# Attention over the scales: the second projection of k and the first of v between the spreads of factors and of weights

## The chip, the cores and the metric

The kernel runs on one core of one Trainium2 chip. The metric is the time of one execution on the device, in microseconds (us). Of the kernel before three executions were timed: the median is 5141.35 us, the lowest 5138.96, the highest 5146.54. Everything is float32.

The engines are named as in the profile: PE is TensorE (matmuls, PEld its weight loads), DVE is VectorE, ACT is ScalarE, POOL is GpSimd.

## What is computed

Four layers follow each other on an image of 2 x 128 channels x 64 x 64: a state-space block with its feed-forward part, two self-attentions over the image's positions, and last an attention over four scales. The change touches this last layer alone. Cut to what matters:

```python
SCALES = (1, 2, 4, 8)
feats = []                                   # four maps of 128 channels, 64 x 64
for i, scale in enumerate(SCALES):
    xs = x if scale == 1 else mean over scale x scale blocks of x
    f = conv3x3(xs, conv_w[i], conv_b[i])
    feats.append(f if scale == 1 else bilinear_resize(f, 64, 64))
xr = stack(feats) as (positions, 4, 128)
q, k, v = split(xr @ attn_in_w.T + attn_in_b)          # 8 heads of 16 channels
attn = softmax(q @ k.T / sqrt(16))                     # 4 x 4 per position and head
o = (attn @ v) @ attn_out_w.T + attn_out_b
res = o + xr
normed = (res - mean(res)) * rsqrt(var(res) + eps) * ln_g + ln_b
out = fus_w @ (the four scales of normed, 512 channels) + fus_b
```

At each of the 8192 positions, four vectors of 128 channels attend to each other, are normalised, and are fused into one.

## The kernel before

The last layer works on items of 512 positions: 2 images x 8 = 16 items. Channels lie on the 128 partitions, positions along the free dimension. The instructions are issued in the order of the program text, each engine works through its own queue in that order, and an engine waits only where it needs what another one has not yet done.

**Items and periods.** `period(n, extra)` is called for n from -2 to 16. One period handles four items at once, each at another step of its way: o = n-1 is fused and written out, p = n gets its weighted sum of v, its output projection and its normalisation factors, m = n+1 gets its scores and its softmax, r = n+2 gets its features, its convolution and its q. What a step does:

- `features(r)` (POOL) builds the three resized scales of `f`; `conv(r, taps)` (PE) and `conv_out(r)` (ACT) build scale 0, in nine matmuls into `pf`.
- `project(i, which, si)` (PE) is one matmul of 128 x 128 by 512 into a buffer `pqkv`. For q (0) and v (2) ACT then copies it to SBUF with its bias; for k (1) it stays in PSUM until `product` reads it. The two k of scales 0 and 1 are made at the end of the period ahead, those of scales 2 and 3 inside this one.
- `product(m, ti)` (DVE) multiplies k of scale ti with q of all four scales into `prod`; `scores(m, ti)` (PE) sums it over the channels of each head into `psc`; `soft_max`, `soft_exp`, `soft_sum` (DVE, ACT, DVE) make the attention weights `at`.
- `weights(p, ti)` (PE, eight short matmuls of 32 rows) spreads the weights of scale ti over the channels into `pw`; `weighted(p, ti)` (DVE) multiplies them with v of scale ti into `ov`; `add_ov` adds the four up (one on POOL, two on DVE).
- `mix_out(p, si)` (PE, then ACT) makes `po`, and from it `sq` and `cen`; `variance` (PE, ACT) and `newton` (DVE, ACT, DVE) make the factors `rs`; `factors(p)` (PE, eight short matmuls of 32 rows) spreads them over the channels into `prs`; `normalise` (DVE, in the next period, where the item is o) multiplies `cen` with them; `fuse(o, ...)` (PE) makes `pfus`, which ACT and a DMA write out as `ot`.

**PSUM.** The eight banks are full. Three hold `mm`, the buffers of one bank that `pqkv`, `pf`, `po` and `pfus` share in turn; one holds `acc` (`psc` and `pva`); four hold the single buffer of tag `pw`, in which `pw` and `prs` replace each other: the weights of an item can be spread only when `normalise` has read the factors of the item ahead. A buffer of a tag is given out again in the order in which the program gave it back.

**SBUF.** v of an item is one tile of 4 x 512 numbers per partition, with one buffer for all items. `prod`, `ov` and `sq` share six buffers.

**The order around the change.** At the end of a period PE does `variance`, then q of scales 0 to 3 of item r, then k of scales 0 and 1 of item r, then `factors(p)`. The next period (in which r has become m, and p has become o) starts on DVE with `product(m, 0)` and `normalise(o)`, on PE with `weights(p, 0)`, k of scale 2, and the first half of `fuse(o)`. The first projection of v stands behind the last scores and `soft_max`, ahead of the last five taps of `conv`; the other three follow the convolution. Some periods carry extra work for the second image: `means` in period 2, coarse convolutions in 3 and 4, `columns` in 5.

In the kernel before, the lines of the profile are these: 1032 is the matmul of `project`, 1039 its copy on ACT, 1045 `product`, 1052 `scores`, 1062 to 1080 the softmax, 1087 `weights`, 1094 `weighted`, 1098 `add_ov`, 1107 and 1108 `mix_out`, 1116 `variance`, 1129 and 1131 `newton`, 1138 `factors`, 1145 `normalise`, 1152 `fuse`, 1005 `conv`. Behind the changed places the line numbers of the kernel after are higher by four.

## Time and profile before

| what | before |
|---|---|
| time, median of three | 5141.35 us |
| span of the profiled execution | 5141.6 us |
| PE busy | 4702.8 us (91%) |
| DVE busy | 4093.2 us (80%) |
| ACT busy | 2367.5 us (46%) |
| POOL busy | 2313.1 us (45%) |
| last layer, 4300 to 5141 us: PE, DVE, ACT, POOL busy | 743.5, 539.5, 242.1, 213.3 us of 841 |
| one `normalise` (DVE, 128 x 2048) | 2.28 us |
| one `product` (DVE, 128 x 2048) | 2.35 us |
| one copy of v (ACT, 128 x 512) | 0.69 us |

Busy time is time in which an engine had an instruction under way. A matmul of float32 appears as two records, one for each pass. The profile also gives the clock granted to PE, as a share of full speed: over the whole span it is 0.941, and in the last layer it is whole or half, in stretches of 3.41 us or multiples of that.

There is one `normalise` in each period, so that the distance from one to the next is the length of a period. In the timeline of DVE they start at 4412.54, 4457.56, 4511.39 (with `means`), 4572.97 and 4624.89 (with coarse convolutions), 4678.66 (with `columns`), 4725.40, 4772.66, 4818.52, 4863.55, 4909.37, 4955.34, 5000.37, 5046.19 and 5087.69 us; the last stands at 5128.94.

### The profile page before, as it was taken

The numbers are of one execution on the slowest core, as the hardware profiler recorded it, in microseconds if no ns is written. First come the engines' busy times: TensorE is split into PE (matmuls) and PEld (weight loads), VectorE is DVE, ScalarE is ACT, GpSimd is POOL, SyncE is SP. The second block draws the span as 40 slices with busy tenths as digits, with TensorE's granted clock in tenths as the row PEclk, the third lists the DMA queues.
The fourth block names the chain that finished last, engine by engine and source line by source line (L and its number), as shares of the span: only waits on it lengthen the run. The fifth ranks groups of instructions, "written<-read, shape, count | busy, mean of one in ns | idle before, by whom it ended". The sixth has DMA issues, their size and how long they took to land.

```text
span 5141.6 us, 48961 instructions
## 1 busy us (share of the span) xinstructions
PE 4702.8 (91%) x14797; PEld 2255.8 (44%) x14797; DVE 4093.2 (80%) x4416; ACT 2367.5 (46%) x3221; POOL 2313.1 (45%) x1948
## 2 busy tenths in 40 slices
PE   5889999999888998789999999999999998899997
PEld 1222222222222222356666666666656665333332
DVE  5999999999999999588878887667767774757665
ACT  4677777777777777322221222333333331232332
POOL 2777777767767777313332233333333333222320
PEclk8898889888999988899999999999999999999998
DMA  5333333333222333124443244444444441000000
GB/s 151 72 68 69 67 69 71 71 71 69 67 68 67 71 73 71 33 63 104 103 105 88 70 103 104 117 99 111 111 99 99 112 112 46 5 5 7 7 5 8
DMA packets 237015, 373.85 MB, mean 73 GB/s; under 512 B 88000, under 2 KB 88400, under 8 KB 228432
## 3 DMA queue, kind: packets, MB, share of 16 engines
q1 hardware_dynamic: 187600, 303.55, 24.9%
q10 hardware_dynamic: 49152, 67.17, 5.5%
q8 instruction: 118, 1.93, 0.2%
q14 instruction: 145, 1.19, 0.1%
HBM read 92.18 MB, written 9.83 MB: 20 GB/s over the span
## 4 chain that ended last, share of the span: by engine, by line
PE 45%; POOL 21%; DVE 13%; issue 11%; ACT 4%; DMA 3%; SPq 2%; ACTq 0%; DVEq 0%; POOLq 0%
POOL h L387 17%; PE po L759 13%; PE pq L709 13%; DVE tr L739 3%; PE pf L1005 2%; DMA pt<-tr 2%; SPq L750 2%; PE pqkv L1032 2%; PE py L399 2%; PE pw L1087 1%; POOL z L410 1%; POOL dtu L347 1%; PE psc L1052 1%; DVE h L384 1%; PE pfus L1152 1%
## 5 line engine op out<-in xcount | busy, mean ns | idle before, releaser
L746 POOL COPY pt<-tr 32x512 f32<-32x512 f32 x1024 | 652.6, 637 | 1499.1 <-DVE tr L739 766.8
L384 DVE TENSOR_TENSOR_SCAN h<-da,carry,h 128x512 f32<-128x512 f32 x1024 | 1241.5, 1266 | 59.1 <-ACT da L373 30.2
L387 POOL TENSOR_TENSOR h<-h,cb 128x2048 f32<-128x2048 f32 x256 | 1161.0, 4535 | 20.9 <-POOL carry L386 0.2
L709 PE MATMUL pq<-k,q 128*128 128x512 f32 x2048 | 963.9, 594 | 8.6 <-DVE sc L714 6.2
L759 PE MATMUL po<-pt,vt 128*128 128x256 f32 x4096 | 967.3, 379 | 2.4 <-DMA pt<-tr 2.4
L724 ACT ACTIVATE sc<-sc,nm 128x2048 f32<-128x2048 f32 x256 | 510.5, 1995 | 925.7 <-DVE nm L720 662.3
L714 DVE TENSOR_SCALAR_CACHE_REDUCE sc<-pq 128x1024 f32<-128x1024 f32 x512 | 624.9, 1222 | 361.5 <-PE pq L709 339.9
L759 PEld LDWEIGHTS po<-pt,vt 128*128 128x128 f32 x4096 | 779.1, 190 | 295.2 <-issue 211.3
L373 ACT ACTIVATE da<-dtb,am 128x512 f32<-128x512 f32 x1024 | 681.5, 684 | 222.4 <-DVE h L384 211.4
L739 DVE STREAM_TRANSPOSE tr<-sc 128x2048 f32<-128x2048 f32 x256 | 591.6, 2311 | 68.5 <-DMA pt<-tr 61.8
L366 DVE TENSOR_TENSOR h<-bb,pdu 128x2048 f32<-128x2048 f32 x256 | 581.7, 2272 | 77.4 <-PE py L399 29.3
L399 PE MATMUL py<-h,sel 128*32 128x512 f32 x2048 | 510.8, 642 | 1.6 <-POOL h L387 1.6
L709 PEld LDWEIGHTS pq<-k,q 128*128 128x128 f32 x2048 | 383.6, 190 | 286.7 <-issue 247.7
L360 PE MATMUL pdu<-dtu,fsel 128*128 128x512 f32 x512 | 327.0, 725 | 101.7 <-DVE h L366 101.6
L399 PEld LDWEIGHTS py<-h,sel 128*32 128x32 f32 x2048 | 115.0, 117 | 416.0 <-issue 409.2
L288 PE MATMUL pu<-xn,wu 128*128 128x512 f32 x512 | 244.7, 611 | 2.6 <-ACT xn L278 1.7
L360 PEld LDWEIGHTS pdu<-dtu,fsel 128*128 128x128 f32 x512 | 96.3, 215 | 310.2 <-DVE h L366 186.2
L386 POOL COPY carry<-h 128x4 f32<-128x4 f32 x256 | 47.9, 187 | 387.7 <-DVE h L384 385.9
L1032 PE MATMUL pqkv<-f,ws 128*128 128x512 f32 x384 | 196.0, 636 | 12.3 <-ACT q L1039 6.3
L1094 DVE TENSOR_TENSOR ov<-v,pw 128x2048 f32<-128x2048 f32 x64 | 146.2, 2284 | 60.9 <-PE pw L1087 60.8
L1098 POOL TENSOR_TENSOR ov<-ov 128x2048 f32<-128x2048 f32 x16 | 72.7, 4541 | 253.7 <-DVE ov L1094 253.7
L1016 POOL TENSOR_SCALAR f<-lo 128x256 f32<-128x256 f32 x32 | 27.7, 865 | 324.6 <-PE po L1107 269.6
(241 smaller groups left out, 5408.5 us busy)
## 6 DMA issues: line engine op xcount, KB each, us to landing
pt<-tr SPq DMA_DIRECT2D x2048, 64.0 KB, 2.0
dtb<-dt SPq DMA_DIRECT2D x1024, 64.0 KB, 2.0
pt<-tr ACTq DMA_DIRECT2D x1024, 64.0 KB, 2.2
bb<-dr SPq DMA_DIRECT2D x128, 256.0 KB, 4.7
cb<-dr SPq DMA_DIRECT2D x128, 256.0 KB, 7.7
uw<-ufold SPq DMA_DIRECT2D x14, 576.0 KB, 3.8
xt<-in_x SPq DMA_DIRECT2D x16, 256.0 KB, 5.0
xr<-in_x SPq DMA_DIRECT2D x16, 256.0 KB, 2.9
```

Source lines behind the costliest of these rows:

```text
L360: nc.tensor.matmul(pdu, lhsT=four(s_ % 4), rhs=st[i]["dtu"][:, s_ // 4, :], start=True, stop=True)
L366: nc.vector.tensor_tensor(h, st[i]["bc", 0], pdu.unsqueeze(1).to_broadcast([P, 4, CH]), ALU.mult)
L373: nc.scalar.activation(da, st[i]["dtb", s_], AF.Exp, scale=am[items[i][1]][:, j, gg, m : m + 1])
L384: nc.vector.tensor_tensor_scan(h[:, m, :], da, h[:, m, :], carries[b, l][:, j, gg, m : m + 1], ALU.mult, ALU.add)
L387: nc.gpsimd.tensor_tensor(h, h, st[i]["bc", 1], ALU.mult)
L399: nc.tensor.matmul(py[r : r + 32, :], lhsT=sel, rhs=st[i]["h", s_ + k][:, m, :], start=(m == 0), stop=(m == 3), tile_position=(0, r),)
L709: nc.tensor.matmul(pq[:, i, :], lhsT=st["q", r, grp][:, it * P : (it + 1) * P], rhs=st["k"][:, at : at + CH], start=True, stop=True)
L714: nc.vector.tensor_scalar(dst, pq, 1.0, None, ALU.mult, ALU.max, accum_out=st["mx"][:, c2 : c2 + 1])
L724: nc.scalar.activation(sc, sc, AF.Exp, bias=nm, scale=scale, accum_out=sm[:, hh : hh + 1])
L739: nc.vector.transpose(tr, st.pop(("sc", r, blk, hh)).rearrange("p (t r f) -> p r t f", r=NB, f=32))
L746: nc.gpsimd.tensor_copy(dst, src)
L759: nc.tensor.matmul(st["po", r, grp], lhsT=st["vt"][:, jt, :], rhs=rhs, start=(jt == 0), stop=(jt == N // P - 1))
```

## The change

PE's work stays the same, matmul for matmul; two of them move into the stretch between `factors` of one item and the first `weights` of the next. `factors(p)` now stands ahead of k of scale 1, and v of scale 0 of item m is made at the very start of the period. Since v of scale 0 is then written while all four v of the item ahead are still to be read, v becomes four tiles of 512 numbers with five buffers in all. To save room in SBUF, the maximum of the softmax shares its buffer with the sum.

```diff
@@ project
             name = "qkv"[m]
+            if m == 2:
+                v = st[i]["v", si] = sp.tile([P, CH], F32, name="v", tag="v", bufs=5)
+                nc.scalar.activation(v, pq, AF.Identity, bias=v1("attn_in_b", m))
+                return
             if si == 0:
                 st[i][name] = sp.tile([P, NS, CH], F32, name=name, tag=name)
@@ soft_max
-            mx = sp.tile([P, G4], F32, name="mx4", tag="mx4")
+            mx = sp.tile([P, G4], F32, name="mx4", tag="sm4")
@@ weighted
-            v = st[i]["v"][:, ti : ti + 1, :].to_broadcast([P, NS, CH])
+            v = st[i].pop(("v", ti)).unsqueeze(1).to_broadcast([P, NS, CH])
@@ period
             do(r, features)
+            do(m, project, 2, 0)
             for ti in range(NS):
                 do(m, product, ti)
...
             do(m, soft_max)
-            do(m, project, 2, 0)
             do(r, conv, (4, 5, 6, 7, 8))
...
             do(r, project, 1, 0)
+            do(p, factors)
             do(r, project, 1, 1)
-            do(p, factors)
             more(6)
```

## The prediction

> **What bounds the kernel now.** I read the page first for the engines' shares, then the chain of waits within one period of the last stage, the timeline of TensorE (PE) and VectorE (DVE) over the same period, and last the windows view cut at the edges of the clock records. Only the last stage is touched (from 4299 us on, 842 us of the span); everything ahead of it stays. Page, part 1:

> ```profile
> PE 4702.8 (91%) x14797; PEld 2255.8 (44%) x14797; DVE 4093.2 (80%) x4416; ACT 2367.5 (46%) x3221; POOL 2313.1 (45%) x1948
> ```

> PE is the busiest, but that is a mean over four stages. The chain of waits from 4405 to 4465 us (start, length, engine, tile, line) shows one period of this stage:

> ```profile
> 4409.08 1.16 ACT q L1039 x2
> 4410.25 0.03 issue
> 4410.27 2.35 DVE prod L1045
> 4412.62 2.20 DVE cen L1145
> 4414.83 0.04 issue
> 4414.87 1.18 PE pw L1087 x8
> ...
> 4420.68 1.13 PE pqkv L1032 x2
> ...
> 4432.68 0.99 PE psc L1052 x8
> 4433.68 1.06 PE pqkv L1032 x2
> 4434.73 4.29 PE pf L1005 x10
> 4439.02 2.58 PE pqkv L1032 x6
> ```

> The chain leaves PE for 4.6 us only: q's last eviction on ScalarE (ACT) lets DVE do product 0 and then `normalise` (cen), and only then may the first `weights` run, because pw and prs share one buffer. From 4420.68 on PE carries it without a break to the next q. The row at 4433.68 is v0 (two records: each f32 matmul is two passes); it is on the chain. The timeline of PE, with idle time in brackets:

> ```profile
> 4410.78 1.14 PE L1138 MATMUL prs<-rs,kc 32*128 32x512 f32 x8
> 4414.87 1.14 PE L1087 MATMUL pw<-at,spread 32*128 32x512 f32 x8 [2.95 <-DVE cen L1145]
> 4415.94 1.13 PE L1032 MATMUL pqkv<-f,ws 128*128 128x512 f32 x2
> 4416.90 1.88 PE L1152 MATMUL pfus<-cen,wfus 128*128 128x512 f32 x4
> 4418.71 1.14 PE L1087 MATMUL pw<-at,spread 32*128 32x512 f32 x8
> 4420.68 1.13 PE L1032 MATMUL pqkv<-f,ws 128*128 128x512 f32 x2 [0.83 <-DVE prod L1045]
> ```

> In each period PE stands idle for 2.95 us between the spread of factors (prs) and that of weights (pw). Windows of one clock record each (PE busy is the second number after the window, the granted clock the third from the end):

> ```profile
> 4413.33:4416.74 3.41, 1.87 (x10) 0.80 (x11) 2.15 (x2) 0.00 (x0) 0.00 (x0) 1.00 0.02 5
> 4863.89:4867.30 3.41, 1.42 (x9) 0.61 (x10) 2.15 (x2) 0.00 (x0) 0.00 (x0) 1.00 0.00 0
> 4867.30:4870.71 3.41, 3.41 (x5) 1.35 (x4) 3.41 (x2) 0.00 (x0) 0.00 (x0) 0.50 0.02 5
> 4908.26:4911.67 3.41, 0.49 (x8) 0.00 (x0) 3.38 (x2) 0.00 (x0) 0.38 (x1) 1.00 0.00 0
> 4911.67:4915.09 3.42, 3.39 (x10) 1.35 (x11) 1.24 (x1) 0.00 (x0) 0.00 (x0) 0.50 0.00 0
> 2761.28:2764.69 3.41, 1.50 (x7) 1.25 (x8) 3.31 (x8) 0.74 (x2) 0.00 (x0) 1.00 0.38 148
> ```

> The reader is to see a second cost of that gap. [...] Where the gap straddles an edge (first row, 1.54 idle) the clock stays whole. Where 1.99 us of idleness or more fall into one window (second and fourth row), the next window has half the clock. The window at 2761 (1.92 idle) kept it, and so did one at 4372 with 1.72.

> [...]

> **The change part by part.** I write o, p, m, r for the period's four items, as the code does.

> *k1 behind the factors.* Before, PE does q0 to q3, k0, k1, prs. The last passes of k0 and k1 start at 4409.40 and 4410.26 in the raw records, prs at 4410.78, 0.52 behind k1. Newton's last step on DVE ends at 4409.12 + 0.73 = 4409.85, so prs can start at 4409.93 behind k0. That gains nothing by itself: `normalise` stands behind product 0 on DVE, which waits for q's eviction (4410.24) and ends at 4412.54, as before. k1 is first read by product 1 (4418.28) and runs in the gap, from 4411.00 (prs + 1.07, the distance from pw to k2 above). Cost nothing, hidden by product 0 and `normalise`.

> *v0 in front of the weights.* It follows k1 in the gap: first pass at 4411.96, end of its record 4412.98. pw still starts at 4414.87, so PE waits 1.89 instead of 2.95. Its wait is for a PSUM buffer that q3's eviction freed at 4410.24: met. Its eviction (0.69 on ACT) falls into ACT's idle stretch of 14.52 us ahead of `ot`; nothing is queued behind it that is due. The old place of v0 closes: rows at 4433.61 and 4434.57 are 0.96 apart, of which 0.10 is the exposed first weight load after the score matmuls, which conv then pays. Like matmuls follow each other every 0.86 (4441.44, 4442.29, 4443.15), so 0.86 leaves the chain. What could hold the rest back? `soft_exp` moves with v3 from 4442.22 to 4441.36, and its input is ready at 4439.33; the output matmul needs the last `add_ov` (4437.26) at 4441.4. Slack 2.0 and 4.2 us: all 0.86 arrive.

> *How often.* Period -1 gives only some 0.43, because v0 of the next item now precedes the first weights (4370.78), where PE has no gap. Periods 0 to 13 give 0.86. Period 14 gives 0: there DVE's `add_ov` releases the output matmul (wait of 1.29 at 5073.22). Sum 0.43 + 14 x 0.858 = 12.4 us.

> *Half clock.* From `normalise` to `normalise` an undisturbed period takes 45.03 us (4818.52 to 4863.55, 4955.34 to 5000.37). Periods with half clock behind the gap take 45.86, 47.26, 45.82, 45.97, 45.82; those with extra work in them show the same late starts of `ov` on DVE (0.83 each in 2 and 5, about 2.2 in 14). The excess is 0.83 + 0.83 + 2.23 + 0.83 + 0.79 + 0.94 + 0.79 + 2.2 = 9.4 us. A gap of 1.89 can put at most 1.89 into a window, under the 1.92 that kept the clock. I take the whole 9.4; the low end is 5 (below).

> *Period with `columns`.* There prs waits for a late newton step with k1 before it at half clock: `normalise` starts 1.25 late (4678.66). With k1 behind prs this goes, but k1 and v0 at half clock then delay pw to about 4680.4 instead of 4681.00: 0.6 us.

> *Buffers.* v becomes single tiles, five of them, as four of p are still to be read when v0 of m is written. v was 8 KB a partition and is 10. mx4 shares the buffer of sm4: writer and readers are all on DVE in order, so no other engine is asked. The evictions of v and DVE's reads have the same shapes (0.69 and 2.28 us). All this costs nothing.

> Sum: 12.4 + 9.4 + 0.6 = 22.4 us; 5141.35 - 22.4 = 5119.

> **The rivals.** (1) *The edge of the throttle lies lower.* Record ends are modelled; if the chip counts 1.89 as idle enough, a gap that lies wholly in one window still halves the clock. An undisturbed period would be 44.17 = 13 windows less 0.20, a disturbed one about 45.0, so the phase drifts down by 0.2 and jumps up by 0.63: one period in four to one in two, 3 to 6 of 14 at 0.83, 2.5 to 5 us back. Then 5122 to 5124. For it: 1.89 is near 1.99. (2) *Only v0's place counts*, because halves come as often as before: 12.4 + 0.6, so 5128. Against it: excess over 2 us came from windows with 2.57 and 2.64 idle, which can't occur any more. (3) *The buffers of `mm` turn.* All of pqkv, pfus, pf and po share three PSUM banks. If they went round in turn, v0 would push `pfus` onto k1's bank, and PE would wait for product 1 ahead of the second weights: pfus at 4420.7 instead of 4416.9, the second weights at 4422.5, `ov` 1 at 4423.7 instead of 4420.55, about 2.9 us a period less 0.86, in 13 periods +27: 5168, slower. Against it: in the kernel before, buffers are given out in the order of their release (pfus takes k0's bank, conv takes pfus's, and only k3 waits for product 1, 0.83), and v0's bank is released ahead of k0's, so k2 gets v0's and pfus k0's again. (4) *Something else ends the period*, gain under 0.2%: about 5138. Against it: the slacks above.

> **How the numbers follow.** Main forecast 0.50 (5119); rival 1 0.20, rival 2 0.14, rival 4 0.07, rival 3 0.09. The three runs of before lie between 5138.96 and 5146.54, so I put 5 to 6 us below the forecast and 4 above rival 2: 5113 to 5132, which leaves out rivals 3 and 4 (0.16). 0.2% is 10.3 us, so faster is 0.84, same 0.07, slower 0.09.

> **What would show it.** In the profile after: k1 and v0 between prs and pw, 1.9 us idle before pw in place of 2.95; `normalise` to `normalise` 44.2 us in nearly every plain period; no half clock behind the gap from 4400 to 5050 us, but still around `means`, `columns` and the tail; conv directly behind the last scores; the start of `ov` no later than before. Wrong if pfus or k2 shows a wait, if periods stay at 45, or if halves stay as frequent.

## The result, and the profile after

The kernel after takes 5119.27 us (median of four executions, 5117.63 to 5119.84); the kernel before, run beside it, 5140.95 (four, 5138.96 to 5146.54). The ratio is 0.9956, with a 95% interval of 0.9938 to 0.9973. The profiled execution spans 5118.0 us, and 5141.6 before. Page of the kernel after, part 1:

```profile
PE 4685.8 (92%) x14797; PEld 2250.5 (44%) x14797; DVE 4091.4 (80%) x4416; ACT 2366.8 (46%) x3221; POOL 2312.5 (45%) x1948
```

The counts are the same; PE is busy for 17 us less, 14 of them in the last layer, since a matmul lasts longer at half clock (in the trace of before, two such records of `pqkv` take 2.08 us at half clock, at 4683.02, and 1.12 at whole clock, at 4688.52), and half clock has become rarer (66.1 us of it from 4290 us to the end of the span, 103.6 before). The chain of waits over one period (start, length, engine, tile, line) has lost one row:

```profile
4408.60 1.17 ACT q L1043 x2
4409.77 0.03 issue
4409.79 2.35 DVE prod L1049
4412.14 2.20 DVE cen L1149
4414.34 0.04 issue
4414.39 1.19 PE pw L1091 x8
...
4420.20 1.13 PE pqkv L1032 x2
...
4432.20 0.99 PE psc L1056 x8
4433.19 4.49 PE pf L1005 x10
4437.68 2.57 PE pqkv L1032 x6
```

Conv (`pf`) follows the last scores directly; the v0 that stood between them is gone. The timeline of PE shows where it went:

```profile
4409.44 1.14 PE L1142 MATMUL prs<-rs,kc 32*128 32x512 f32 x8
4410.52 1.98 PE L1032 MATMUL pqkv<-f,ws 128*128 128x512 f32 x4
4414.39 1.14 PE L1091 MATMUL pw<-at,spread 32*128 32x512 f32 x8 [1.89 <-DVE cen L1149]
4415.46 1.13 PE L1032 MATMUL pqkv<-f,ws 128*128 128x512 f32 x2
4416.42 1.88 PE L1156 MATMUL pfus<-cen,wfus 128*128 128x512 f32 x4
4418.23 1.14 PE L1091 MATMUL pw<-at,spread 32*128 32x512 f32 x8
4420.20 1.13 PE L1032 MATMUL pqkv<-f,ws 128*128 128x512 f32 x2 [0.83 <-DVE prod L1049]
```

k1 and v0 (four records, two matmuls) fill part of the gap, which is now 1.89 us. Neither k2 nor `pfus` waits; k3 has the same 0.83 as before. The clock windows (width, PE busy second, granted clock third from the end) tell the rest:

```profile
4802.69:4806.11 3.42, 1.53 (x8) 0.47 (x10) 3.21 (x2) 0.69 (x1) 0.20 (x1) 1.00 0.00 0
4806.11:4809.52 3.41, 3.41 (x10) 1.09 (x11) 1.52 (x1) 0.00 (x0) 0.00 (x0) 0.50 0.00 0
4935.81:4939.23 3.42, 1.57 (x4) 0.38 (x2) 3.40 (x2) 0.69 (x1) 0.39 (x1) 1.00 0.00 0
4939.23:4942.64 3.41, 3.37 (x14) 1.37 (x14) 2.17 (x1) 0.00 (x0) 0.00 (x0) 1.00 0.00 0
```

With 1.89 us idle in one window (3.42 - 1.53) the next one still ran at half clock; with 1.85 it did not. A period of 44.16 is 13 windows less 0.21, so the gap moves against the windows by that much each time. From the period that starts at 4759.46 to the one at 4981.10, the largest part of it inside one window is 1.84, 1.89, 1.43, 1.65, 1.85 and 1.89. In two plain periods the whole gap lay in one window, the one that starts at 4803.62 and the one at 4981.10, and behind these two the clock was halved.

The distance from one `normalise` to the next, from DVE's timelines, shows where the 23.6 us between the two profiled spans went (the medians are 21.7 apart). Ahead of the first q of the last layer nothing changed (it starts at 4341.41 before, at 4341.70 after); from there to the end it is 800.2 us before and 776.3 after, 23.9 less.

| stretch (number of the period's first `normalise`) | before | after | gain |
|---|---|---|---|
| first q to first `normalise` | 71.13 | 70.36 | 0.77 |
| 1, 3, 4, 12, none with half clock behind the gap in either | 45.02, 61.59, 51.91, 45.03 | 44.16, 60.72, 51.05, 44.16 | 0.86 or 0.87 each |
| 2 | 53.83 | 52.09 | 1.74 |
| 5 (ends with the late start after `columns`) | 53.77 | 50.77 | 3.00 |
| 6 (behind `columns`) | 46.74 | 44.47 | 2.27 |
| 7, 8 | 47.26, 45.86 | 44.16, 44.16 | 3.10, 1.70 |
| 9 | 45.03 | 44.99 | 0.04 |
| 10, 11 | 45.82, 45.97 | 44.16, 44.16 | 1.66, 1.81 |
| 13 | 45.82 | 44.97 | 0.85 |
| 14 | 41.51 | 40.48 | 1.03 |
| 15 and the rest to the end | 53.88 | 51.47 | 2.41 |

In period 14 the gap ahead of the weights no longer halves the clock, but another wait does: that for the last `add_ov`, ahead of the second output matmul. PE reaches it 0.86 earlier, since v0 is gone from the way there, and so it waits 2.15 instead of the 1.29 of the kernel before, all of it in one window. Its row in the timeline of PE, and two windows:

```profile
5050.83 1.12 PE L1112 MATMUL po<-ov,wc 128*128 128x512 f32 x2 [2.15 <-DVE ov L1102]
5048.46:5051.88 3.42, 1.27 (x4) 0.57 (x4) 3.36 (x3) 0.09 (x1) 0.00 (x0) 1.00 0.00 0
5051.88:5055.29 3.41, 3.41 (x6) 1.35 (x5) 2.57 (x4) 1.78 (x3) 0.00 (x0) 0.50 0.01 2
```

### The profile page after: what moved, and what is told of

Same layout as the page of the kernel before. It is cut to its first block, busy times and chain, and to the rows that moved or that the text cites. A ratio compares the mean times of both kernels' runs of the same rounds, so it can differ in the third digit from the quotient of the medians.

```text
span 5118.0 us, 48991 instructions
## 1 busy us (share of the span) xinstructions
PE 4685.8 (92%) x14797; PEld 2250.5 (44%) x14797; DVE 4091.4 (80%) x4416; ACT 2366.8 (46%) x3221; POOL 2312.5 (45%) x1948
## 3 DMA queue, kind: packets, MB, share of 16 engines
q8 instruction: 118, 1.93, 0.2%
## 4 chain that ended last, share of the span: by engine, by line
PE 47%; POOL 19%; DVE 13%; issue 10%; DMA 4%; ACT 3%; SPq 2%; ACTq 0%; DVEq 0%; POOLq 0%
POOL h L387 15%; PE po L759 13%; PE pq L709 13%; DVE tr L739 3%; PE pf L1005 3%; DMA pt<-tr 2%; PE py L399 2%; SPq L750 2%; PE pqkv L1032 1%; PE pu L288 1%; DVE prod L1049 1%; DVE h L384 1%; PE psc L1056 1%; PE pw L1091 1%; POOL dtu L347 1%
## 5 line engine op out<-in xcount | busy, mean ns | idle before, releaser
L1032 PE MATMUL pqkv<-f,ws 128*128 128x512 f32 x384 | 189.9, 620 | 11.5 <-DVE prod L1049 9.9
```

## The experiments

The theory: v0's place gives 0.86 a period, because PE then carries the chain for one matmul less, and the shorter gap gives more where it no longer halves the clock. Against it stood that the order of `factors` does the work; that half clock is a thing beside the gap and costs the path nothing; and that something else soon ends the period.

### `factors` alone

The kernel before, with the order of `factors` and k1 changed and v0 left in its old place:

```diff
             do(r, project, 1, 0)
-            do(r, project, 1, 1)
             do(p, factors)
+            do(r, project, 1, 1)
```

> Kernel before, with the factors moved ahead of k1 and v0 left where it was. My theory (two costs: v0 on PE's chain, and half clock after an idle gap of 1.89 us or more inside one window): k1 moves from one side of prs to the other, the gap before pw only shrinks from 2.95 to about 2.75 us, plain periods stay at 45.0 or 45.8 to 47.3 us; the period with columns gets about 1 us shorter. 5137 to 5142 us. Rival A (the order of factors and k1 is what frees the chain, since normalise waits for prs): periods near 44.2, 5125 or less.

Measured: 5142.36 us (13 executions, 5135.31 to 5146.27) beside 5142.84 for the kernel before (28): ratio 0.9996, 0.9988 to 1.0004; this is the upper end of what was expected. The timeline of PE:

```profile
4814.33 1.13 PE L1032 MATMUL pqkv<-f,ws 128*128 128x512 f32 x2
4818.21 2.05 PE L1087 MATMUL pw<-at,spread 32*128 32x512 f32 x8 [2.75 <-DVE cen L1145]
```

k1 now stands behind the factors, and the gap is still 2.75: PE reaches it sooner, but the weights wait for `normalise`, which waits for product 0. Undisturbed periods take 45.02. The order of `factors` is not what gains. Two of its windows, each with the next, belong to the question of the clock:

```profile
4770.54:4773.96 3.42, 1.57 (x9) 0.61 (x10) 2.16 (x2) 0.00 (x0) 0.00 (x0) 1.00 0.00 0
4773.96:4777.37 3.41, 3.41 (x5) 1.35 (x4) 3.41 (x2) 0.00 (x0) 0.00 (x0) 0.50 0.00 0
4627.16:4630.58 3.42, 1.64 (x10) 0.64 (x11) 2.16 (x2) 0.00 (x0) 0.00 (x0) 1.00 0.00 0
4630.58:4633.99 3.41, 3.41 (x6) 1.28 (x4) 3.41 (x2) 0.00 (x0) 0.00 (x0) 0.50 0.00 0
```

Here 1.85 and 1.78 us idle were enough to halve the clock, where 1.85 was not in the kernel after.

### v0 alone

The kernel after, with `factors` back behind k1:

```diff
             do(r, project, 1, 0)
-            do(p, factors)
             do(r, project, 1, 1)
+            do(p, factors)
```

> Kernel after, with the factors back behind k1, so that v0 alone stands between prs and pw. My theory: the two matmuls ahead of pw end where they ended, the gap is again 1.89 us, plain periods are 44.2 us; only the period with columns loses about 1 us: 5119 to 5122 us. Rival A (the order of factors is needed): 5130 or more.

Measured: 5123.06 us (5 executions, 5122.02 to 5124.42), ratio 0.9961, 0.9948 to 0.9973; 1 us above what was expected. The timeline of PE:

```profile
4806.99 1.14 PE L1091 MATMUL pw<-at,spread 32*128 32x512 f32 x8 [1.89 <-DVE cen L1149]
```

The gap and the plain periods (44.17) are those of the kernel after. The period that ends behind `columns` takes 52.11 instead of 50.77, and the next gives 0.30 of it back (44.17 instead of 44.47), so the order of `factors` is worth about 1.0 us, once, in this pair of profiles. Of the 3.3 us between the two spans (5121.3 and 5118.0) 2.6 lie in the last period and the end, where both have the same code.

### The gap filled with matmuls that nobody needs

The kernel before, with v0 in its old place, and k1's matmul repeated twice behind the factors, into the buffer in which it already stands:

```diff
+        def again(i, si):
+            at = WS_IN + C
+            nc.tensor.matmul(st[i]["k", si], lhsT=ws[:, at : at + C], rhs=st[i]["f"][:, si, :], start=True, stop=True)
...
             do(p, factors)
+            do(r, again, 1)
+            do(r, again, 1)
```

> Kernel before, with the matmul of k1 repeated twice into the same buffer behind the factors, so that PE does more work, all of it in the gap, and v0 stays on the chain. My theory: the gap before pw shrinks from 2.95 to about 1.0 us, no window behind it is at half clock any more, plain periods are 45.0 us without exception; gain about 9 us, less up to 3 in the period with columns: 5130 to 5135 us. Rival B (half clock is absorbed by waits of other engines, and the gain is all v0's place): 5141 or more.

Measured: 5134.09 us (16 executions, 5127.22 to 5137.66), ratio 0.9981, 0.9974 to 0.9989. The timeline of PE, the second row being the repeats:

```profile
4812.16 1.14 PE L1142 MATMUL prs<-rs,kc 32*128 32x512 f32 x8
4813.23 1.98 PE L1044 MATMUL pqkv<-f,ws 128*128 128x512 f32 x4
4816.25 1.14 PE L1091 MATMUL pw<-at,spread 32*128 32x512 f32 x8 [1.03 <-DVE cen L1149]
```

The windows view over seven and a half periods, of the kernel before and of this one:

```profile
4700.00:5040.00 340.00, 317.51 (x1077) 110.62 (x1076) 229.91 (x150) 112.06 (x177) 92.36 (x91) 0.97 0.02 6
```

```profile
4700.00:5040.00 340.00, 326.94 (x1116) 114.26 (x1116) 232.54 (x153) 115.90 (x183) 92.25 (x91) 1.00 0.02 6
```

PE does more, and the kernel is faster: nothing left the chain, but the clock is whole (1.00) where it was 0.97. Every period from 6 to 13 takes 45.02 to 45.04, and period 14 takes 39.33 instead of 41.51. So half clock behind the gap was a cost on the path. The gains in periods 2 to 14 come to 10.5 us, 7.8 of them in periods 7 to 14; 1.6 is lost at the start, where there is no gap to fill (72.77 instead of 71.13).

### A second v in the gap

The kernel after, with v1 behind v0 at the start of the period; v has six buffers, and two tiles used only ahead of the periods share the softmax's small buffer:

```diff
-    v = ... sp.tile([P, CH], F32, name="v", tag="v", bufs=5)
+    v = ... sp.tile([P, CH], F32, name="v", tag="v", bufs=6)
...
             do(m, project, 2, 0)
+            do(m, project, 2, 1)
...
-            for si in range(1, NS):
+            for si in range(2, NS):
                 do(m, project, 2, si)
```

> Kernel after, with v1 as well behind v0 in the gap (six buffers of v; two small tiles of the preparation share the buffer of sm4 to make room). My theory: v1 must wait for ACT to empty v0's buffer, starts about 0.8 us behind v0's end and is through just as pw may start; the chain loses another 0.86 us a period and no half clock is left in plain periods: periods of 43.3 us, 5104 to 5109 us. Rival C (the gap holds no more, pw slips behind v1 and its eviction): periods of 44 us or more, 5116 or more.

Measured: 5111.12 us (5 executions, 5108.60 to 5111.78), ratio 0.9937, 0.9924 to 0.9951. The profiled execution took 5108.6, inside what was expected; the median is 2 us above it. The timeline of PE:

```profile
4409.94 1.14 PE L1142 MATMUL prs<-rs,kc 32*128 32x512 f32 x8
4411.01 2.84 PE L1032 MATMUL pqkv<-f,ws 128*128 128x512 f32 x6
4414.89 1.14 PE L1091 MATMUL pw<-at,spread 32*128 32x512 f32 x8 [1.03 <-DVE cen L1149]
```

k1, v0 and v1 run without a break, so the wait of v1 for v0's eviction that was expected does not occur, and the gap is 1.03. Plain periods take 43.30, again 0.86 less (44.16 - 43.30), and none has half clock. The step repeats, so nothing else was yet close to ending the period. No run splits v into single tiles and leaves v0 in its old place; but v is split in this kernel and in the kernel after alike, and the step between them is again that of one matmul's place. One window in period 14, ahead of the output matmuls, has 1.93 us idle (3.42 - 1.48), and yet the clock behind it stayed whole:

```profile
5037.18:5040.60 3.42, 1.48 (x4) 0.77 (x5) 3.35 (x4) 0.00 (x0) 0.00 (x0) 1.00 0.00 0
```

### `normalise` ahead of product 0

The gap is there because DVE does product 0 first. The kernel after, with the two exchanged:

```diff
             do(m, project, 2, 0)
+            do(o, normalise)
             for ti in range(NS):
                 do(m, product, ti)
-                if ti == 0:
-                    do(o, normalise)
```

> Kernel after, with normalise ahead of product 0 on DVE. My theory: the gap before pw is made by product 0 and normalise standing in line on DVE, and normalise needs prs only (ready 1.1 us behind the start of prs). Then normalise starts at prs's end, pw may start 1.4 us earlier, the gap shrinks from 1.89 to about 0.5 us and no half clock is left behind it; but the first ov still has to wait for product 0, so that the period gains only about 0.55 us, 44.16 to 43.6: 5108 to 5113 us. Rival D (product 0 coming later holds up pfus and k3, which take the buffers of k0 and k1): periods of 44.2 us or more, 5117 or more.

Measured: 5113.53 us (5 executions, 5111.31 to 5114.26), ratio 0.9945, 0.9932 to 0.9957. The timeline of PE:

```profile
4411.36 1.14 PE L1091 MATMUL pw<-at,spread 32*128 32x512 f32 x8 [0.50 <-DVE cen L1149]
...
4415.81 1.14 PE L1091 MATMUL pw<-at,spread 32*128 32x512 f32 x8 [0.21 <-DVE ov L1098]
4418.07 1.12 PE L1032 MATMUL pqkv<-f,ws 128*128 128x512 f32 x2 [1.12 <-DVE prod L1049]
```

The gap falls from 1.89 to 0.50, but a period only from 44.16 to 43.67, and the median lies half a us above what was expected. From factors to weights it is 1.40 shorter (3.55 instead of 4.95); from the weights to the next factors 0.91 longer (40.12 instead of 39.21), because product 0 and all behind it on DVE now come later against PE: 0.21 ahead of the second weights, and 1.12 instead of 0.83 ahead of k3.

### All of `fuse` ahead of the second weights

If PE waits for DVE there, work that needs nothing from DVE belongs there. The kernel just shown, with all four matmuls of `fuse` behind the first weights:

```diff
-                if ti < 2:
-                    do(o, fuse, (2 * ti, 2 * ti + 1))
-                else:
+                if ti == 0:
+                    do(o, fuse, (0, 1, 2, 3))
+                elif ti > 1:
                     do(r, conv, (2 * ti - 4, 2 * ti - 3))
```

> As e5_normalise_first, with all four matmuls of fuse at once ahead of the second weights. My theory: PE's idle stretch ahead of k3, in which it waits for product 1, takes the second half of fuse off the chain; the second weights come about 1.3 us later, the chain loses 1.7 us a period against the kernel after: periods of about 42.5 us, 5088 to 5097 us. Rival E (the later second weights hold DVE up, and the period ends with DVE's adds and the softmax): 43.6 us or more, 5108 or more.

Measured: 5098.68 us (5 executions, 5096.64 to 5099.94), ratio 0.9915, 0.9902 to 0.9929. It is the fastest of these kernels, some 20 us below the kernel after, and 1 to 2 us above what was expected. The timeline of PE:

```profile
4414.79 3.70 PE L1156 MATMUL pfus<-cen,wfus 128*128 128x512 f32 x8
4418.43 1.14 PE L1091 MATMUL pw<-at,spread 32*128 32x512 f32 x8
4419.50 1.12 PE L1032 MATMUL pqkv<-f,ws 128*128 128x512 f32 x2
...
4421.97 1.14 PE L1091 MATMUL pw<-at,spread 32*128 32x512 f32 x8 [0.36 <-DVE ov L1098]
...
4426.43 1.14 PE L1091 MATMUL pw<-at,spread 32*128 32x512 f32 x8 [0.40 <-DVE ov L1098]
```

k3 no longer waits. Two smaller waits for `ov` stand ahead of the third and fourth weights (0.36 and 0.40), and a period takes 42.90 instead of the 42.5 expected.

The same edit on the kernel with two v in the gap, and `normalise` behind product 0:

> As e4_two_v, with all four matmuls of fuse at once ahead of the second weights. My theory: the same idle stretch of 0.83 us ahead of k3 is filled, the second weights come later by 1.7, the chain loses about 0.9 us a period against e4: periods of about 42.4 us, 5094 to 5101 us. Rival E as before: 43.3 us or more, 5109 or more.

Measured: 5106.29 us (5 executions, 5105.42 to 5106.97), ratio 0.9931, 0.9919 to 0.9943; periods of 43.11, where 42.4 was hoped for, and a time 5 us above what was expected. The timelines of PE and of DVE:

```profile
4416.72 3.60 PE L1156 MATMUL pfus<-cen,wfus 128*128 128x512 f32 x8
4420.24 1.14 PE L1091 MATMUL pw<-at,spread 32*128 32x512 f32 x8
...
4423.79 1.14 PE L1091 MATMUL pw<-at,spread 32*128 32x512 f32 x8 [0.36 <-DVE ov L1098]
```

```profile
4421.45 2.29 DVE L1098 TENSOR_TENSOR ov<-v,pw 128x2048 f32<-128x2048 f32 x1 [1.01 <-PE pw L1091]
```

With two v PE did not wait at the second weights before this edit. The longer `fuse` delays them, DVE waits 1.01 for them, and PE later waits for DVE: k3's wait of 0.83 is exchanged for 0.76 of others (0.36 and 0.40, as in the kernel above). With `normalise` first, PE did wait there, 0.21, and 1.12 ahead of k3, and the same edit brought these 1.33 down to 0.76. It is worth 0.77 a period there (43.67 to 42.90), and 0.19 here (43.30 to 43.11). That the waits make the difference is read from the four traces; the two pairs differ in the place of `normalise` and in the number of v moved.

## Why the prediction was right, and which step was wrong

The time predicted was 5119, the time measured 5119.27. The mechanism held, but that the sum of 22.4 came so close is partly luck: a term that was too large met gains that had not been foreseen. The amounts below are those of the two profiled executions.

- *v0's place*: predicted 12.4, measured 12.0. Periods 1, 3, 4 and 12 show 0.86 or 0.87 with no half clock on either side, which for the 13 periods comes to 11.2; the start gave 0.77, not 0.43 + 0.86 = 1.29. Zero in period 14 was right: with no half clock ahead of its output matmuls it takes 39.33 both with v0 in its old place (the filled gap) and with it moved (two v). What v0's place frees there becomes a longer wait for `add_ov`: 1.29 in the filled gap, 2.15 in the kernel after, 3.01 with two v. Why the start gave less than predicted was not looked into.
- *k1 behind the factors*: cost nothing and gained nothing by itself, as `factors` alone shows. Behind `columns` it gave about 1.0 where 0.6 had been put.
- *Buffers*: no new wait in the trace of the kernel after, so the rival with PSUM buffers in turn (5168) fell. With two v, too, v1 runs directly behind v0. That rival was not tried by forcing the order of buffers.
- *Half clock* is the step that failed. It was said that a gap of 1.89 puts at most 1.89 into a window, under the 1.92 (1.91 by the row shown) that kept the clock, and so the whole 9.4 was taken. But 1.89 halved the clock twice in the kernel after, for 0.83 and 0.81, and once with v0 alone. And in period 14 the sum took back all 2.2 of half clock, though the wait of 1.29 that it named there grows by the 0.86 of v0 to 2.15, above its own edge of 1.99; that half clock cost 1.15 (40.48 instead of 39.33). What the table gives for half clock, with 0.86 taken off where v0 counts: 0.88 in period 2, 2.24, 0.84, -0.82, 0.80, 0.95 and -0.01 in periods 7 to 11 and 13, 1.03 in 14, together 5.9; and in period 5 3.00 - 0.86 = 2.14, which holds both its half clock and the order of `factors`. That is 8.0, where 9.4 + 0.6 = 10.0 had been predicted. On this point the rival with the lower edge was right. It put one period in four to one in two; there were two in 13, but once the gap had drifted into one window the second came four periods behind the first, as the rival's drift of 0.2 a period and jump of 0.63 have it.
- *Not foreseen*: 2.27 - 0.86 = 1.4 in period 6, since the half clock behind `columns` lasted 13.65 us before and 6.83 after; and 2.4 in the last period and the end. There no code changed. In the six traces that keep `fuse` and `normalise` as they were, that period takes 38.93, 39.92, 40.60, 40.79, 41.25 and 41.38 us, and in the same order PE worked at half clock in it for 9.5, 13.7, 15.0, 15.4, 15.6 and 15.9 us (the kernel after has the first of each, the kernel before the fifth). So this too goes with half clock, through the way the waits of the tail fall into the windows; no run was made to move them there.

So 12.0 + 8.0 + 1.4 + 2.4 = 23.8 of the 23.9 us. That only v0's place counts (5128) fell with the filled gap; that something else ends the period (5138) fell with two v.

## What to carry to other kernels

Work whose inputs are ready early belongs into a wait that PE cannot avoid, and what it is worth is read at its old place: one float32 matmul of 128 x 128 by 512 off the chain gave 0.86 us a period, twice in a row. A gap can cost more than its length, through the clock: in the kernel after, plain periods took 44.16 us, and 44.99 and 44.97 where half clock stood behind the gap. Since the windows did not keep step with the periods (44.16 us is 13 windows less 0.21), that cost fell on two of 13 periods, and had to be priced as a share of them, not as all or nothing. Time that is freed ahead of another wait makes that wait longer: in period 14 it went from 1.29 to 2.15 us, and half clock then stood behind it. Before work is moved past a wait, see which of the two engines is behind at that point: the same exchange in `fuse` was worth 0.77 us a period where PE waited for DVE, and 0.19 where it did not and DVE came to wait for PE.

## What the runs showed of the hardware

In the traces of before and after, every record of the clock between the first and the last is a whole number of windows of 3.413 us long. There is no single length of idleness that halves the clock in these traces. Idle time inside one window of 3.41 us kept it at 1.72 and 1.91 (before), 1.85 (after) and 1.93 (two v), and halved it at 1.78 and 1.85 (`factors` alone), 1.89 (after) and 1.99 (before). The ends of matmuls are modelled, and idle time is not all that counts. In the first layer of the kernel before, a window without idle time left the next one at half clock; matmuls of 8 rows (`pt`) took up much of it. Two windows, and two rows of the timeline of PE:

```profile
552.85:556.27 3.42, 3.42 (x7) 0.88 (x6) 3.42 (x4) 3.40 (x7) 1.11 (x1) 1.00 0.10 24
556.27:559.68 3.41, 1.87 (x4) 0.34 (x4) 3.31 (x3) 3.37 (x5) 1.25 (x1) 0.50 0.98 219
553.05 1.12 PE L335 MATMUL pt<-dbl,wd 8*128 8x512 f32 x2
555.16 1.12 PE L335 MATMUL pt<-dbl,wd 8*128 8x512 f32 x2
```

Matmuls that compute nothing new made the kernel faster, by a ratio of 0.9981 (0.9974 to 0.9989), because they kept the clock whole (1.00 from 4700 to 5040 us, where it was 0.97).
